# The last of 64 graphs: its transpose moved to TensorE, its steps put in a new order, its result stored by row tile

## The chip, the cores and the metric

One core of a Trainium2 chip. The metric is the device time of one execution in microseconds (us). Times below are medians of 3 to 9 executions. "Span" is the time from the first to the last instruction in the one execution that was profiled; the device time of that same execution is about 1.8 us longer.

## The reference, cut to what matters

64 graphs of 256 nodes with 512 features, f32. Two layers, each with a residual and a layer norm. In the second, a softmax over the 256 nodes of a graph scales the rows of `v`.

```python
def _L0_gnn_ref(x, adj, W):
    deg = jnp.sum(adj, axis=-1, keepdims=True)
    agg = jnp.einsum('bij,bjf->bif', adj, x) / jnp.maximum(deg, EPS)
    cat = jnp.concatenate([x, agg], axis=2)
    return jax.nn.relu(jnp.einsum('bnf,of->bno', cat, W))

def _L1_gnn_ref(X, adj, mask, Wqk, Wv):
    q, k = jnp.split(X @ Wqk, 2, axis=-1)
    v = X @ Wv
    agg = jnp.einsum('bij,bjd->bid', adj, k * mask[:, :, None])
    w = inv_scale * mask * jnp.einsum('bid,bid->bi', q, agg)
    return jax.nn.softmax(w, axis=1)[:, :, None] * v

x = _layernorm(x + _L0_gnn_ref(x, adj, L0_gnn_W), axis=-1)
x = _layernorm(x + _L1_gnn_ref(x, adj, nodemask, L1_gnn_Wqk, L1_gnn_Wv), axis=-1)
```

## The kernel before

Each product of matrices is done in Strassen's way with 7 block products (A11B11, A12B21, S1T1, S2T2, S3T3, S4B22, A22T4) in place of 8. The graphs are pipelined: in iteration i the first layer of graph i, the gather with the adjacency of graphs i and i-1, and the second layer's products of graph i-2 are woven together; graph i-4 is finished. The second layer needs the normalized rows `x1` transposed. That is done by 32x32 block transposes on VectorE and 16 small transfers that put the blocks in place:

```python
    def transpose_rows(src, dst):
        sq = pool.tile([P, P // Q, NF, NT, Q], F32, name="sq", bufs=1)
        for t in range(NT):
            nc.vector.transpose(sq[:, :, :, t, :].rearrange("p b c q -> p c b q"), src[:, t, :])
        to = dst.rearrange("f c (t a q) -> f (c t) a q", t=NT, q=Q)
        for a in range(P // Q):
            for b in range(P // Q):
                nc.sync.dma_start(to[b * Q:(b + 1) * Q, :, a, :],
                                  sq[a * Q:(a + 1) * Q, b].rearrange("p c t q -> p (c t) q"))

    def layer1_steps(g):
        # ... seven products; the first one is copied to q by ScalarE before its dot,
        #     the scores are complete only with the sixth (A22T4):
        u = bank()
        product(u, s["A11"], w["B11"])
        nc.scalar.copy(q, u)
        dot(q, 0, part)
        # ... S1T1, S2T2, A12B21, S3T3 ...
        product(u, s["A22"], w["T4"], start=False)
        dot(u, 1, sc[:, 1:2])
        product(p5, s["S4"], w["B22"], start=False)
        nc.vector.tensor_add(v[:, 0, :], p5, v[:, 0, :])

    def finish(g):
        x1, v, p = x1s.pop(g), vs.pop(g), probs.pop(g)
        o = pool.tile([P, NT, F], F32, name="o")
        for t in range(NT):
            nc.vector.scalar_tensor_tensor(o[:, t, :], v[:, t, :], p[:, t:t + 1], x1[:, t, :],
                                           op0=OP.mult, op1=OP.add)
        layer_norm(o, o)
        nc.sync.dma_start(out[g].rearrange("(t p) f -> p t f", p=P), o)

    for i in range(B + LAG - 1):
        # ...
        if i - 3 >= B - 2:            # the last two graphs: scores turned by TensorE, softmax on one row
            softmax_turned(i - 3)
            finish(i - 3)
        # ...
```

In all other iterations the 16 transfers have time: those of graph 61 are issued from 1886.82 to 1897.22 us, and its `x1T` is first read at 1909.0, without a wait. For graph 63, the last, nothing is left to do meanwhile.

Of the kernel before, what the change touches and what calls it, by code (L numbers as in the profile page):

```python
# [35 lines left out]
F32 = mybir.dt.float32  # L36
AF = mybir.ActivationFunctionType
OP = mybir.AluOpType
AX = mybir.AxisListType

P = 128
Q = 32
LAG = 4
# [5 lines left out]
def resnorm_kernel(  # L49
# [12 lines left out]
    nc = tc.nc  # L62
    B, N, F = x.shape
    A = wqk_t.shape[0] // 2
    NT, NF, NA = N // P, F // P, A // P
    H, HF = NF // 2, F // 2
# [5 lines left out]
    pool = ctx.enter_context(tc.tile_pool(name="pool", bufs=2))  # L72
    small = ctx.enter_context(tc.tile_pool(name="small", bufs=4))
# [28 lines left out]
    with setup as sp:  # L102
        wqk = sp.tile([P, 2 * NA, F], F32, name="wqk")
        for a in range(NA):
            src = wqk_t.rearrange("(h a p) f -> a p h f", p=P, h=2)[a]
# [14 lines left out]
        ident = const.tile([P, P], F32, name="ident")  # L120
        make_identity(nc, ident)
        eps = const.tile([P, 1], F32, name="eps")
# [23 lines left out]
    def row_sums(aT, eng):  # L146
# [8 lines left out]
        eng.tensor_sub(s4, a12, s2)  # L155
        return {"A11": a11, "A12": a12, "A22": a22, "S1": s1, "S2": s2, "S3": s3, "S4": s4}

    def product(ps, a, b, start=True):
        for c in range(H):
            nc.tensor.matmul(ps, a[:, c, :], b[:, c, :], start=start and c == 0, stop=(c == H - 1),  # L160
                             skip_group_check=True)

    def bank():
        return ps_mm.tile([P, F], F32, name="mm")
# [11 lines that stand above are left out]
                                  sq[a * Q:(a + 1) * Q, b].rearrange("p c t q -> p (c t) q"))  # L176

    def layer_norm(src, dst):
        mv = small.tile([P, NT, 2], F32, name="mv")
        for t in range(NT):  # L180
            st = small.tile([P, 6], F32, name="st")
            nc.vector.bn_stats(st, src[:, t, :])  # L182
            nc.vector.bn_aggr(mv[:, t, :], st)  # L183
        rstd = small.tile([P, NT], F32, name="rstd")
        nc.scalar.activation(rstd, mv[:, :, 1], AF.Ln, bias=eps)  # L185
        nc.scalar.activation(rstd, rstd, AF.Exp, scale=-0.5)
        for t in range(NT):
            nc.vector.tensor_scalar(dst[:, t, :], src[:, t, :], mv[:, t, 0:1], rstd[:, t:t + 1],  # L188
                                    op0=OP.subtract, op1=OP.mult)

# [105 lines left out]
    def norm0(g):  # L296
        x1s[g] = pool.tile([P, NT, F], F32, name="x1", bufs=LAG + 2)
        layer_norm(owns.pop(g), x1s[g])
        for t in range(NT):
            nc.scalar.activation(values(g + 1)[:, 1, t, :], x1s[g][:, t, :], AF.Copy,  # L300
                                 scale=mask_sb[:, t, g:g + 1])
        x1Ts[g] = pool.tile([P, NF, N], F32, name="x1T")
        transpose_rows(x1s[g], x1Ts[g])

    def turn(g):
        sums1[g] = row_sums(x1Ts.pop(g), nc.vector)
# [1 line left out]
    def layer1_steps(g):  # L308
        sc, part = scores[g] = (small.tile([P, NT], F32, name="scores", bufs=3),
                                small.tile([P, 1], F32, name="part", bufs=3))  # L310
        s, w, agg = sums1.pop(g), W1, aggs.pop(g + 1)[:, 1]
        v = vs[g] = late.tile([P, NT, F], F32, name="v", bufs=LAG)
        q = pool.tile([P, F], F32, name="q")

        def dot(a, t, to):
            nc.vector.scalar_tensor_tensor(q, a, 1.0, agg[:, t, :], op0=OP.mult, op1=OP.mult, accum_out=to)  # L316
# [5 lines that stand above are left out]
        yield  # L322
        p5 = bank()
        product(p5, s["S1"], w["T1"])
        yield
        product(u, s["S2"], w["T2"], start=False)
        nc.scalar.copy(v[:, 0, :], u)  # L327
        yield
        p2 = bank()
        product(p2, s["A12"], w["B21"])  # L330
        dot(p2, 0, sc[:, 0:1])
        yield
        product(u, s["S3"], w["T3"], start=False)
        nc.scalar.copy(v[:, 1, :], u)  # L334
        nc.vector.tensor_add(v[:, 1, :], p5, v[:, 1, :])
        yield
        product(u, s["A22"], w["T4"], start=False)
        dot(u, 1, sc[:, 1:2])
        yield
        product(p5, s["S4"], w["B22"], start=False)  # L340
        nc.vector.tensor_add(v[:, 0, :], p5, v[:, 0, :])  # L341
        yield

    def scale_scores(g, to):
        w, part = scores.pop(g)
        nc.vector.tensor_add(w[:, 0:1], w[:, 0:1], part)
        nc.vector.scalar_tensor_tensor(to, w, inv_scale, mask_sb[:, :, g], op0=OP.mult, op1=OP.mult)

    def write_scores(g):
# [12 lines left out]
    def softmax(g):  # L362
        w, row = columns.pop(g), rowsW.pop(g)
        top = small.tile([P, 1], F32, name="top")
        nc.vector.reduce_max(top, row, axis=AX.X, negate=True)
        total = small.tile([P, 1], F32, name="total")
        nc.scalar.activation(row, row, AF.Exp, bias=top, accum_out=total)
        p = probs[g] = small.tile([P, NT], F32, name="probs", bufs=2)
        nc.scalar.activation(p, w[:, :NT], AF.Exp, bias=top)
        nc.vector.reciprocal(total, total)  # L370
        nc.vector.tensor_scalar(p, p, total, None, op0=OP.mult)

    def softmax_turned(g):
        w = small.tile([P, NT], F32, name="w", bufs=2)
        scale_scores(g, w)
        wr = bank()[:1, :N]
        for t in range(NT):
            nc.tensor.transpose(wr[:, t * P:(t + 1) * P], w[:, t:t + 1], ident)
        top = small.tile([1, 1], F32, name="top1", bufs=2)
        nc.vector.reduce_max(top, wr, axis=AX.X, negate=True)  # L380
        e = small.tile([1, N], F32, name="e", bufs=2)
        total = small.tile([1, 1], F32, name="total1", bufs=2)
        nc.scalar.activation(e, wr, AF.Exp, bias=top, accum_out=total)
        nc.vector.reciprocal(total, total)
        nc.vector.tensor_scalar(e, e, total, None, op0=OP.mult)
        ps = bank()[:, :NT]
        for t in range(NT):
            nc.tensor.transpose(ps[:, t:t + 1], e[:, t * P:(t + 1) * P], ident[:1, :1])
        probs[g] = small.tile([P, NT], F32, name="probs", bufs=2)
        nc.vector.tensor_copy(probs[g], ps)  # L390

    def finish(g):
        x1, v, p = x1s.pop(g), vs.pop(g), probs.pop(g)
# [6 lines that stand above are left out]
# [4 lines left out]
        for _ in range(n):  # L404
            next(gen, None)

    for i in range(B + LAG - 1):
        new = i < B
        if i + 2 < B:
            with tc.issue_after(loaded.ins):  # L410
                loaded = load(i + 2)
        if i == 1:
            W1 = weight_sums(w1, "t1_")
        if 0 <= i - 3 < B - 2:
            write_scores(i - 3)
            read_scores(i - 3)
        if new:
            began, added = layer0_a(i)
        if 0 <= i - 2 < B:
            turn(i - 2)  # L420
        l1 = layer1_steps(i - 2) if 0 <= i - 2 < B else iter(())
        step(l1)
        if new:
            layer0_b(i)
        if i - 3 >= B - 2:
            softmax_turned(i - 3)
            finish(i - 3)
        if i <= B:
            z, summed = gather_a(i)
        step(l1, 2)  # L430
        step(z)
        if 0 <= i - LAG < B - 2:
            with tc.issue_after(began.ins), tc.issue_after(added.ins):
                softmax(i - LAG)
            with tc.issue_after(summed.ins):
                finish(i - LAG)
        for _ in range(4):
            step(l1)
            step(z)
        if new:  # L440
            combine0(i)
            norm0(i)
        if i + 1 < B:
            with tc.issue_after(began.ins), tc.issue_after(added.ins):
                prepare(i + 1)
# [26 lines left out]
```

## Time and profile before

| what | before |
|---|---|
| device time, median of the first 3 runs | 1988.32 us (1986.9 to 1988.72); in all later comparisons medians of 1987.68 to 1988.52 |
| span of the profiled run | 1986.5 us |
| TensorE busy | 99% |
| part of the span that the change can reach | the last 43 us |

How to read the lines in this document. A timeline line has start (us), length (us), engine, source line, operation, output<-input, shapes, count of instructions merged into it; in brackets the idle time of the engine just before it and what ended it. PE is TensorE, PEld its weight loads, DVE VectorE, ACT ScalarE, POOL GpSimd, SPq the queue that issues transfers. One f32 block product shows as two MATMUL instructions, so a Strassen product of two blocks is "x4". Numbers of source lines are those of the kernel that ran: L160 of the kernel before is L162 of the changed one.

For the end of the kernel I count from the start of the last gather's first product (`mm<-vals,adj`, at 1945.97 here), and call that "after the gather". The kernel before: last product ends at 29.6, last combination of softmax and residual starts at 32.4, end at 40.5.

### The profile page before, as it was taken

What the parts mean: (1) busy time and instruction counts of PE and PEld (TensorE: products, weight loads), DVE (VectorE), ACT (ScalarE), POOL (GpSimd) and SP (SyncE); (2) the same over time, 40 slices, a digit from 0 to 9 for tenths busy, and PEclk for the clock granted to TensorE, in tenths of its full rate; (3) what the DMA queues carried; (4) which work ended last, traced back from release to release, by engine and by line L of the source; (5) the groups of instructions that cost most, each with busy time, mean ns of one, the idle gap of its engine ahead of it and who ended that gap; (6) DMA issues with size and microseconds to landing.
All of it is one profiled execution on the core that took longest, in us unless ns stands there. A gap on an engine that the chain in (4) does not pass through costs nothing.

```text
span 1986.5 us, 19676 instructions
## 1 busy us (share of the span) xinstructions
PE 1960.3 (99%) x5416; PEld 1017.5 (51%) x5416; DVE 1566.5 (79%) x3218; ACT 650.0 (33%) x1543; POOL 419.6 (21%) x518
## 2 busy tenths in 40 slices
PE   8999999999999999999999999999999999999996
PEld 3554555555555545555555555555555555555552
DVE  5677877888788788778878887887787788878877
ACT  2323333333233333333332333333333333323332
POOL 3122221221221221222212212212222122122100
PEclk9999999999999999999999999999999999999999
DMA  6333333333333333333333333333333333333221
GB/s 223 88 83 82 98 94 85 95 91 90 96 80 100 93 83 103 93 81 95 91 90 95 83 98 94 83 102 93 81 95 92 89 96 81 101 96 80 80 45 56
DMA packets 394830, 182.62 MB, mean 92 GB/s; under 512 B 285793, under 2 KB 359393, under 8 KB 394721
## 3 DMA queue, kind: packets, MB, share of 16 engines
q1 hardware_dynamic: 394720, 181.36, 34.0%
q8 instruction: 44, 0.72, 0.2%
q14 instruction: 66, 0.53, 0.1%
HBM read 114.10 MB, written 33.62 MB: 74 GB/s over the span
## 4 chain that ended last, share of the span: by engine, by line
PE 96%; DVE 1%; SPq 1%; DMA 0%; ACT 0%; issue 0%; DVEq 0%
PE mm L160 76%; PE mm L259 19%; SPq L175 1%; PE mm L131 1%; DVE st L182 0%; DMA adj<-adj_t 0%; DMA wqk<-wqk_t 0%; DVE own L293 0%; DVE own L291 0%; DMA x1T<-sq 0%; DVE x L188 0%; DVE o L396 0%; ACT vals L300 0%; DVE v L341 0%; DVE t L141 0%
## 5 line engine op out<-in xcount | busy, mean ns | idle before, releaser
L160 PE MATMUL mm<-w,s 128*128 128x512 f32 x1024 | 481.5, 592 | 0.8 <-ACT v L327 0.8
L160 PE MATMUL mm<-t,s 128*128 128x512 f32 x1024 | 461.4, 593 | 0.2 <-ACT q L320 0.2
L160 PEld LDWEIGHTS mm<-t,s 128*128 128x128 f32 x1024 | 194.7, 190 | 243.7 <-issue 228.2
L160 PEld LDWEIGHTS mm<-w,s 128*128 128x128 f32 x1024 | 194.2, 190 | 192.8 <-issue 155.0
L160 PE MATMUL mm<-w,x1T 128*128 128x512 f32 x512 | 241.4, 594 | 3.9 <-DMA x1T<-sq 3.9
L160 PE MATMUL mm<-w,xT 128*128 128x512 f32 x512 | 240.9, 592 | 0.0
L201 POOL TENSOR_TENSOR sa<-adj 128x128 f32<-128x128 f32 x64 | 45.8, 716 | 760.2 <-PE mm L259 758.7
L152 POOL TENSOR_TENSOR s<-xT 128x256 f32<-128x256 f32 x64 | 46.8, 731 | 706.3 <-PE mm L160 687.3
L259 PE MATMUL mm<-tv,sa 128*128 128x256 f32 x768 | 187.4, 379 | 0.6 <-DVE tv L249 0.4
L259 PEld LDWEIGHTS mm<-tv,sa 128*128 128x128 f32 x768 | 145.7, 190 | 76.3 <-issue 48.2
L233 DVE TENSOR_TENSOR vals<-mm,vals 128x512 f32<-128x512 f32 x64 | 44.2, 691 | 142.9 <-PE mm L160 142.9
L185 ACT ACTIVATE rstd<-mv,eps 128x2 f32<-128x2 f32 x128 | 37.9, 296 | 341.3 <-DVE mv L183 341.3
L160 PEld LDWEIGHTS mm<-w,x1T 128*128 128x128 f32 x512 | 97.2, 190 | 98.9 <-issue 95.6
L160 PEld LDWEIGHTS mm<-w,xT 128*128 128x128 f32 x512 | 97.3, 190 | 94.7 <-issue 91.4
L327 ACT COPY v<-mm 128x512 f32<-128x512 f32 x64 | 37.5, 586 | 284.8 <-PE mm L160 284.8
L160 PE MATMUL mm<-t,xT 128*128 128x512 f32 x256 | 126.8, 617 | 2.8 <-ACT vals L222 2.8
L160 PE MATMUL mm<-t,x1T 128*128 128x512 f32 x256 | 125.4, 612 | 0.9 <-ACT v L334 0.9
L291 DVE SCALAR_TENSOR_TENSOR own<-zr,rdeg,own 128x512 f32<-128x512 f32 x128 | 107.6, 841 | 22.0 <-ACT zr L281 21.9
L259 PE MATMUL mm<-vals,adj 128*128 128x256 f32 x512 | 121.3, 379 | 1.9 <-DVE vals L233 1.9
L259 PEld LDWEIGHTS mm<-vals,adj 128*128 128x128 f32 x512 | 97.1, 190 | 43.6 <-issue 16.7
L215 ACT COPY own<-mm 128x512 f32<-128x512 f32 x64 | 37.5, 586 | 227.4 <-PE mm L160 227.4
L316 DVE SCALAR_TENSOR_TENSOR q<-mm,zr 128x512 f32<-128x512 f32 x128 | 86.1, 673 | 32.4 <-PE mm L160 32.4
(89 smaller groups left out, 2729.5 us busy)
## 6 DMA issues: line engine op xcount, KB each, us to landing
xT<-x_t SPq DMA_DIRECT2D x64, 512.0 KB
x<-x SPq DMA_DIRECT2D x64, 512.0 KB
x1T<-sq SPq DMA_DIRECT2D x1024, 32.0 KB
out<-o SPq DMA_DIRECT2D x64, 512.0 KB
adj<-adj_t SPq DMA_DIRECT2D x64, 256.0 KB
rows<-adj SPq DMA_DIRECT2D x64, 256.0 KB
row<-d SPq DMA_DIRECT2D x62, 128.0 KB
d<-turned SPq DMA_DIRECT2D x248, 0.2 KB
```

Of the source, the lines that this page charges most:

```text
L131: nc.tensor.matmul(ps[c], wqk[:, a, c * P:(c + 1) * P], wqk[:, NA + a, :], start=(a == 0), stop=(a == NA - 1))
L152: eng.tensor_add(s1, a21, a22)
L160: nc.tensor.matmul(ps, a[:, c, :], b[:, c, :], start=start and c == 0, stop=(c == H - 1), skip_group_check=True)
L175: nc.sync.dma_start(to[b * Q:(b + 1) * Q, :, a, :], sq[a * Q:(a + 1) * Q, b].rearrange("p c t q -> p (c t) q"))
L185: nc.scalar.activation(rstd, mv[:, :, 1], AF.Ln, bias=eps)
L201: nc.gpsimd.tensor_add(sa[:, 0], a21, a22)
L215: began = nc.scalar.copy(own[:, 0, :], u)
L233: nc.vector.tensor_add(y[:, 0, :], p5, y[:, 0, :])
L259: nc.tensor.matmul(ps[:, k * HF:(k + 1) * HF], sumsA[g - k][a], w[b][:, n, :], start=start and n == 0, stop=True, skip_group_check=True)
L291: nc.vector.scalar_tensor_tensor(own[:, t, :], z[:, t, :], rdeg[:, t:t + 1], own[:, t, :], op0=OP.mult, op1=OP.add)
L316: nc.vector.scalar_tensor_tensor(q, a, 1.0, agg[:, t, :], op0=OP.mult, op1=OP.mult, accum_out=to)
L327: nc.scalar.copy(v[:, 0, :], u)
```

## The change

Its intent: let TensorE transpose the last x1 so that no transfer is waited for; do the products that the scores need first (A11B11, A12B21, S2T2, A22T4, S3T3), so that the softmax runs beside the rest; normalize and store the last two row tiles one by one.

```diff
@@ norm0
         x1Ts[g] = pool.tile([P, NF, N], F32, name="x1T")
-        transpose_rows(x1s[g], x1Ts[g])
+        if g < B - 1:
+            transpose_rows(x1s[g], x1Ts[g])
+
+    def turn_last(g):
+        for t in range(NT):
+            ps = bank()
+            for c in range(NF):
+                nc.tensor.transpose(ps[:, c * P:(c + 1) * P], x1s[g][:, t, c * P:(c + 1) * P], ident)
+            copy = nc.scalar.copy if t else nc.vector.tensor_copy
+            copy(x1Ts[g][:, :, t * P:(t + 1) * P], ps.rearrange("p (c n) -> p c n", c=NF))
@@ new
+    def layer1_last(g):
+        # ... set-up, dot() cut
+        u, p2, p3, p4, p5 = (bank() for _ in range(5))
+        product(u, s["A11"], w["B11"])
+        dot(u, 0, part[:, 0:1])
+        with tc.issue_after(queued[0]):
+            e = softmax_rows(g - 1)
+        product(p2, s["A12"], w["B21"])
+        dot(p2, 0, sc[:, 0:1])
+        with tc.issue_after(queued[0]):
+            probs[g - 1] = softmax_cols(e)
+        finish(g - 1)
+        product(u, s["S2"], w["T2"], start=False)
+        nc.scalar.copy(v[:, 0, :], u)
+        product(p4, s["A22"], w["T4"])
+        dot(p4, 1, part[:, 1:2])
+        product(u, s["S3"], w["T3"], start=False)
+        dot(u, 1, sc[:, 1:2])
+        nc.scalar.copy(v[:, 1, :], u)
+        product(p3, s["S4"], w["B22"])
+        with tc.issue_after(queued[0]):
+            e = softmax_rows(g)
+        nc.vector.tensor_add(v[:, 0, :], p3, v[:, 0, :])
+        product(p5, s["S1"], w["T1"])
+        for t in range(NT):
+            nc.vector.tensor_add(v[:, t, :], p5, v[:, t, :])
+        with tc.issue_after(queued[0]):
+            p = softmax_cols(e)
+        for t in range(NT):
+            ot = o[:, t:t + 1, :]
+            nc.vector.scalar_tensor_tensor(ot[:, 0], v[:, t, :], p[:, t:t + 1], x1[:, t, :],
+                                           op0=OP.mult, op1=OP.add)
+            layer_norm(ot, ot)
+            nc.sync.dma_start(out[g, t * P:(t + 1) * P, :], ot[:, 0])
@@ main loop (cut): one iteration fewer; turn_last(B - 1) in iteration B, layer1_last(B - 1) in iteration B + 1
```

In the build that ran, the scheduler put S3T3 ahead of A22T4. Not shown: `product` remembers its last instruction in `queued`, `layer_norm` takes one tile or two, `softmax_turned` is cut into `softmax_rows` and `softmax_cols`.

More of the change, by code (lines that the diff above doesn't have):

```diff
@@ L156, in row_sums @@
         return {"A11": a11, "A12": a12, "A22": a22, "S1": s1, "S2": s2, "S3": s3, "S4": s4}
+    queued = [None]
     def product(ps, a, b, start=True):
         for c in range(H):
-            nc.tensor.matmul(ps, a[:, c, :], b[:, c, :], start=start and c == 0, stop=(c == H - 1),
-                             skip_group_check=True)
+            queued[0] = nc.tensor.matmul(ps, a[:, c, :], b[:, c, :], start=start and c == 0,
+                                         stop=(c == H - 1), skip_group_check=True).ins
     def bank():
@@ L178, in layer_norm @@
     def layer_norm(src, dst):
+        n = src.shape[1]
         mv = small.tile([P, NT, 2], F32, name="mv")
-        for t in range(NT):
+        for t in range(n):
             st = small.tile([P, 6], F32, name="st")
@@ L184, in layer_norm @@
         rstd = small.tile([P, NT], F32, name="rstd")
-        nc.scalar.activation(rstd, mv[:, :, 1], AF.Ln, bias=eps)
-        nc.scalar.activation(rstd, rstd, AF.Exp, scale=-0.5)
-        for t in range(NT):
+        nc.scalar.activation(rstd[:, :n], mv[:, :n, 1], AF.Ln, bias=eps)
+        nc.scalar.activation(rstd[:, :n], rstd[:, :n], AF.Exp, scale=-0.5)
+        for t in range(n):
             nc.vector.tensor_scalar(dst[:, t, :], src[:, t, :], mv[:, t, 0:1], rstd[:, t:t + 1],
@@ L342, in layer1_steps, with dot @@
         yield
+    def layer1_last(g):
+        sc, part = scores[g] = (small.tile([P, NT], F32, name="scores", bufs=3),
+                                small.tile([P, NT], F32, name="parts", bufs=1))
+        s, w, agg, x1 = sums1.pop(g), W1, aggs.pop(g + 1)[:, 1], x1s.pop(g)
+        v = late.tile([P, NT, F], F32, name="v", bufs=LAG)
+        o = pool.tile([P, NT, F], F32, name="o")
+        q = pool.tile([P, F], F32, name="q")
+        def dot(a, t, to):
+            nc.vector.scalar_tensor_tensor(q, a, 1.0, agg[:, t, :], op0=OP.mult, op1=OP.mult, accum_out=to)
+        u, p2, p3, p4, p5 = (bank() for _ in range(5))
[30 more added lines that the diff above has]
+            nc.sync.dma_start(out[g, t * P:(t + 1) * P, :], ot[:, 0])
     def scale_scores(g, to):
         w, part = scores.pop(g)
-        nc.vector.tensor_add(w[:, 0:1], w[:, 0:1], part)
+        n = part.shape[1]
+        nc.vector.tensor_add(w[:, :n], w[:, :n], part)
         nc.vector.scalar_tensor_tensor(to, w, inv_scale, mask_sb[:, :, g], op0=OP.mult, op1=OP.mult)
@@ L371, in softmax, with softmax_rows @@
         nc.vector.tensor_scalar(p, p, total, None, op0=OP.mult)
-    def softmax_turned(g):
+    def softmax_rows(g):
         w = small.tile([P, NT], F32, name="w", bufs=2)
@@ L385, in softmax_turned, with softmax_cols @@
         nc.vector.tensor_scalar(e, e, total, None, op0=OP.mult)
+        return e
+    def softmax_cols(e):
         ps = bank()[:, :NT]
@@ L388, in softmax_turned @@
             nc.tensor.transpose(ps[:, t:t + 1], e[:, t * P:(t + 1) * P], ident[:1, :1])
-        probs[g] = small.tile([P, NT], F32, name="probs", bufs=2)
-        nc.vector.tensor_copy(probs[g], ps)
+        p = small.tile([P, NT], F32, name="probs", bufs=2)
+        nc.vector.tensor_copy(p, ps)
+        return p
     def finish(g):
@@ L405, in step @@
             next(gen, None)
-    for i in range(B + LAG - 1):
+    for i in range(B + LAG - 2):
         new = i < B
@@ L420, in resnorm_kernel @@
             turn(i - 2)
-        l1 = layer1_steps(i - 2) if 0 <= i - 2 < B else iter(())
+        l1 = layer1_steps(i - 2) if 0 <= i - 2 < B - 1 else iter(())
         step(l1)
@@ L424, in resnorm_kernel @@
             layer0_b(i)
-        if i - 3 >= B - 2:
-            softmax_turned(i - 3)
-            finish(i - 3)
+        if i - 3 == B - 2:
+            with tc.issue_after(summed.ins):
+                softmax(i - LAG)
+                finish(i - LAG)
+            layer1_last(B - 1)
         if i <= B:
@@ L431, in resnorm_kernel @@
         step(z)
-        if 0 <= i - LAG < B - 2:
+        if 0 <= i - LAG < B - 3:
             with tc.issue_after(began.ins), tc.issue_after(added.ins):
@@ L436, in resnorm_kernel @@
                 finish(i - LAG)
+        if i == B:
+            with tc.issue_after(queued[0]):
+                turn_last(B - 1)
         for _ in range(4):
```

## The prediction

The sum stands as it was forecast: 4.1 us, 4.0 after the price of the transposes, so 1984.3, and 1984.5 with 0.2 net for rival (a). Cut are (a)'s comparison of its wait with an idle time that no run had shown, and the terms of rival (b); the 1.6 us upward in the range is (a)'s 0.9 with the cut term of (b). That 0.9 and its chance of a third are estimates: the slow products of the trace are 0.77 and 0.59 us longer than warm ones. So is the 0.22 us for a transpose, from the measured pace of 0.215 us.

> **What bounds the kernel now.** I read the page first, then the chain that ended last, then the last 40 us in order of time.
>
> ```profile
> PE 1960.3 (99%) x5416; PEld 1017.5 (51%) x5416; DVE 1566.5 (79%) x3218; ACT 650.0 (33%) x1543; POOL 419.6 (21%) x518
> PE 96%; DVE 1%; SPq 1%; DMA 0%; ACT 0%; issue 0%; DVEq 0%
> ```
>
> TensorE is busy for 99% of the span and carries 96% of the chain. The change does not touch its 64 graphs of matmuls: the order of instructions of the changed build is the same on all engines until graph 63, the last, has been normalized by its first layer, about 1943.4 us into a span of 1986.5. So at most the last 43 us, 2.2% of the span, can move, and most of that is work that stays. The stretches there (busy time of each engine, count, clock, DMA share, GB/s):
>
> ```profile
> core 0: us, PE busy (x) PEld busy (x) DVE busy (x) ACT busy (x) POOL busy (x), PEclk, DMA share, GB/s
> 1945.00:1959.50 14.50, 10.42 (x30) 5.50 (x30) 10.11 (x27) 3.57 (x9) 0.00 (x0) 1.00 0.27 50
> 1959.50:1975.90 16.40, 15.43 (x34) 5.75 (x34) 12.98 (x35) 3.51 (x10) 0.00 (x0) 0.90 0.17 62
> 1975.90:1986.50 10.60, 0.29 (x3) 0.20 (x2) 5.24 (x13) 1.06 (x4) 0.00 (x0) 0.75 0.23 86
> ```
>
> Three losses: TensorE idle for 4 of the first 14.5 us; a clock of 0.90 in the second stretch; no matmul at all in the last 10.6 us. The timeline names them:
>
> ```profile
> 1944.95 1.29 DVE L171 STREAM_TRANSPOSE sq<-x 128x512 f32<-128x512 f32 x2
> 1946.31 11.59 SPq L175 DMA_DIRECT2D x1T<-sq  x16
> 1955.08 0.59 PE L259 MATMUL mm<-vals,sa 128*128 128x256 f32 x2
> 1959.55 2.65 PE L160 MATMUL mm<-w,x1T 128*128 128x512 f32 x4 [3.87 <-DMA x1T<-sq]
> 1962.87 2.57 PE L160 MATMUL mm<-t,s 128*128 128x512 f32 x4 [0.25 <-ACT q L320]
> 1967.40 1.88 PE L160 MATMUL mm<-w,x1T 128*128 128x512 f32 x4
> 1971.67 1.98 PE L160 MATMUL mm<-t,x1T 128*128 128x512 f32 x4 [0.68 <-ACT v L334]
> 1973.63 1.98 PE L160 MATMUL mm<-w,s 128*128 128x512 f32 x4
> 1975.65 0.69 DVE L341 TENSOR_TENSOR v<-mm,v 128x512 f32<-128x512 f32 x1 [0.17 <-PE mm L160]
> 1978.38 1.41 DVE L396 SCALAR_TENSOR_TENSOR o<-v,probs,x 128x512 f32<-128x512 f32 x2
> 1981.81 1.00 DVE L188 TENSOR_SCALAR o<-o,mv,rstd 128x512 f32<-128x512 f32 x2 [0.60 <-ACT rstd L186]
> ```
>
> The transpose of x1 goes through VectorE and 16 small transfers, issued in 11.59 us; TensorE runs out of other work at 1955.67 and waits 3.87 us. Then eight matmul instructions take 2.65 and 2.57 us where the same form takes 1.88 warm: (2.65-1.88)+(2.57-1.98) = 1.4 us, and the two small transposes among them 0.64 against 0.38, so some 1.6 us of slow clock. At the end VectorE and ScalarE work alone: from the last matmul's end at 1975.61, softmax, normalization and store take 10.9 us.
>
> [...]3.87 us of idle, then slow matmuls. [...]No full f32 block is transposed here before; the nearest row is a 128x128 weight load, 190 ns, at a pace of 0.215 us where 256-column matmuls follow it. [...]The chain shows 1.95 us from the last x1T issue to its landing, and 3.69 us from the last normalization's end (1982.81) to the end of the span, of which about 1.4 move the 512 KB.
>
> **The change part by part.** I took the new order of each engine and its waits and added durations from the trace, from 1944.24 (TensorE has its last product before the part that differs). The same addition of the old order lands within 0.1 us of the trace at 1955.7, and again from the end of the slow clock to the last normalization, so the method is good to about that.
>
> 1. Removed: the two VectorE transposes (1.29 us), the 16 issues, the 3.87 us wait, the 1.6 us of slow clock, and one ScalarE copy (0.59).
> 2. Added on TensorE: 8 transposes. With 0.22 us each[...], 1.8 us at 1946.7, behind the two gather products (1945.85 to 1946.7), fully on TensorE's path. The copies out, one on VectorE (taken as the 0.69 of an addition from PSUM) and one on ScalarE (0.59), lie beside the next product and gathers: VectorE's ends at 1950.7, and the first product of the last graph wants it at 1952.3.
> 3. The products now follow without a gap. From 1948.4: graph 62's product (2 x 0.86), gathers and remaining products of 62 with half a product of 63 to 1957.4 (small waits for ScalarE's copies, 0.1 to 0.3), rest of that product, scores of 62 turned at 1958.3, then A12B21 and S2T2 to 1961.95.
> 4. New waits on TensorE. The product S3T3 adds into the bank that ScalarE copies first: copy at 1962.1, start at 1962.75, 0.8 us lost. Then it waits for the scaled exponentials of 62 (0.3, at 1964.9). Then S4B22 is streamed by 1968.55, and the next instruction in its order, the turn of 63's scores, waits for VectorE. VectorE still has graph 62 to finish: probabilities at 1965.4, two combinations (0.66 each to the next), statistics (0.60 each), a dot (0.60), the v addition, two normalizations (0.45 each), the second dot (0.67), two small ones; scores at 1971.3. TensorE stands 2.8 us.
> 5. The last product S1T1 then runs 1971.6 to 1973.45 beside the maximum, exponential and scaling of 63's scores (done 1973.3). Before, its counterpart ended at 1975.61: 2.2 us earlier.
> 6. From the last product: two additions of 0.61 and a copy to 1974.9 (the small transposes of e are ready before), two combinations to 1976.3, statistics to 1977.5, aggregates to 1977.7, ScalarE twice two small ones (one more pair than before, half overlapped) to 1978.35, normalizations ending 1978.9 and 1979.4. That is 5.9 us where the old chain took 7.2 (1975.61 to 1982.81): the first combination starts 1.4 us after the last product in place of 2.8, and from there on the two are equal.
> 7. Stores by row tile: the first 256 KB leave 0.45 us before the second, and the last transfer carries half: of the 3.69 us tail I take off 0.6 (an estimate: half of the 1.4 us of moving).
>
> Sum: 2.2 + 1.3 + 0.6 = 4.1 us. The transposes at 0.22 rather than the 0.21 that I added with cost 0.1. The span was 1986.5 where the median is 1988.32, so 1.8 us lie outside it, taken as unchanged: 1988.3 - 4.0 = 1984.3.
>
> **The rivals.** (a) Slow clock at the new wait. [...]If the clock falls, the last product takes up to 0.9 us longer and its end is on the path: about 1985.1. I weigh this with a third, +0.3 us. The old trace speaks for a drop only after 3.87 us, and against one after the 0.68 at 1971.67. (b) The transposes cost more than a weight load each[...] (c) VectorE takes the place of the DMA as the bound: already in step 4, as 12 us of nearly unbroken VectorE from 1958.5 to 1971.3; any VectorE row 10% longer adds up to 1 us. (d) Nothing is gained, because the 3.87 us wait just moves behind graph 62's finish: 1988. Against it: the addition has 63's products start 7 us earlier, at 1952.3 against 1959.55, and the wait left is 2.8. (e) More is gained, if VectorE's queue of graph 62 waits less than I think: the floor is TensorE's work without waits, about 3.5 us less: 1981.
>
> **Range and chances.** From (a) I add 0.2 net: predicted 1984.5. Runs before spread over 1.8 us; (a) and (b) together could put it 1.6 up, (e) some 2 down. 1982.3 to 1986.7 should hold it 8 times in 10. Two per cent is 40 us, about all that is not shared work, so within 2%: 0.985; faster 0.01, slower 0.005.
>
> **What would show each step.** Transposes at 0.22 us in a row at about 1946.7 and no x1T transfer in the last 40 us (1, 2); no TensorE wait over 1 us between 1948 and 1962, clock 1.00 there (3); a wait of 2 to 3.5 us before the turn of the last scores, released by VectorE, and the shorter one for ScalarE's v copy (4); about 6 us from the last product to the last normalization (6); about 3.1 from there to the end (7). Wrong would be: slow matmuls after the transposes[...], or a store tail that stays at 3.7.

## The result, and the profile after

The change took 1983.99 us (median of 6 runs, 1983.78 to 1984.69) where the kernel before took 1988.52 (6 runs, 1986.9 to 1990.27). The ratio is 0.9978 (95% interval 0.9965 to 0.999). Ratios here are the mean time of one kernel's runs over that of the other's of the same rounds, so not quite the ratio of these medians. That is 4.5 us, 0.2%: "the same" by a threshold of 2%, but clear of noise.

The page of the changed kernel, busy time and chain:

```profile
PE 1959.8 (99%) x5424; PEld 1018.5 (51%) x5424; DVE 1566.7 (79%) x3220; ACT 650.0 (33%) x1545; POOL 419.4 (21%) x518
PE 98%; DVE 1%; DMA 0%; ACT 0%; issue 0%; DVEq 0%
```

The transfer queue (SPq) has left the chain. The same stretches as in the prediction (the last one ends with the span):

```profile
1945.00:1959.50 14.50, 14.50 (x49) 8.11 (x48) 13.48 (x36) 4.47 (x13) 0.00 (x0) 1.00 0.10 38
1959.50:1975.90 16.40, 11.23 (x26) 4.03 (x24) 12.45 (x34) 2.96 (x10) 0.00 (x0) 0.90 0.17 64
1975.90:1982.80 6.90, 0.00 (x0) 0.00 (x0) 3.20 (x8) 0.71 (x4) 0.00 (x0) 0.62 0.20 76
```

TensorE (first pair of numbers) now fills the first stretch and has gaps in the second, whose clock is 0.90 again. The last stretch, without products, went from 10.6 to 6.9 us. The timeline, in the same places as before:

```profile
1946.38 1.04 PE L313 MATMUL mm<-ident,x 128*128 128x128 f32 x8
1951.13 1.02 PE L162 MATMUL mm<-w,x1T 128*128 128x512 f32 x2
1961.63 1.98 PE L162 MATMUL mm<-w,s 128*128 128x512 f32 x4 [0.68 <-ACT v L379]
1970.25 0.38 PE L436 MATMUL mm<-ident,w 128*1 128x128 f32 x2 [2.69 <-DVE w L405]
1970.47 3.37 PE L162 MATMUL mm<-t,s 128*128 128x512 f32 x4
1973.88 1.29 DVE L391 TENSOR_TENSOR v<-mm,v 128x512 f32<-128x512 f32 x2 [1.64 <-PE mm L162]
1975.27 1.42 DVE L396 SCALAR_TENSOR_TENSOR o<-v,probs,x 128x512 f32<-128x512 f32 x2
1978.60 1.00 DVE L191 TENSOR_SCALAR o<-o,mv,rstd 128x512 f32<-128x512 f32 x2 [0.51 <-ACT rstd L189]
```

All 8 transposes take 1.04 us. The wait for transfers is gone. A wait of 2.69 us for the last scores has come, and the product behind it takes 3.37 us instead of 1.88: the clock fell here too (0.50 granted from 1970.71 to 1974.13 us). The end comes 37.3 us after the gather, not 40.5.

### The profile page after: what moved, and what is told of

Same layout as the page of the kernel before. It is cut to its first block, busy times and chain, and to the rows that moved or that the text cites. A ratio compares the mean times of both kernels' runs of the same rounds, so it can differ in the third digit from the quotient of the medians.

```text
span 1982.8 us, 19678 instructions
## 1 busy us (share of the span) xinstructions
PE 1959.8 (99%) x5424; PEld 1018.5 (51%) x5424; DVE 1566.7 (79%) x3220; ACT 650.0 (33%) x1545; POOL 419.4 (21%) x518
## 4 chain that ended last, share of the span: by engine, by line
PE 98%; DVE 1%; DMA 0%; ACT 0%; issue 0%; DVEq 0%
PE mm L162 77%; PE mm L262 19%; PE mm L131 1%; DMA wqk<-wqk_t 0%; DMA adj<-adj_t 0%; DVE st L185 0%; ACT vals L303 0%; DVE own L296 0%; ACT vals L225 0%; DVE o L396 0%; DVE vals L236 0%; DVE own L223 0%; DVE t L141 0%; DVE t L140 0%; DVE w L142 0%
## 5 line engine op out<-in xcount | busy, mean ns | idle before, releaser
L262 PEld LDWEIGHTS mm<-vals,adj 128*128 128x128 f32 x512 | 97.1, 190 | 43.6 <-issue 16.9
L328 DVE SCALAR_TENSOR_TENSOR q<-mm,zr 128x512 f32<-128x512 f32 x126 | 84.7, 672 | 32.4 <-PE mm L162 32.4
```

The costliest lines, as they stand in the source:

```text
L262: nc.tensor.matmul(ps[:, k * HF:(k + 1) * HF], sumsA[g - k][a], w[b][:, n, :], start=start and n == 0, stop=True, skip_group_check=True)
L328: nc.vector.scalar_tensor_tensor(q, a, 1.0, agg[:, t, :], op0=OP.mult, op1=OP.mult, accum_out=to)
```

## The experiments

Twelve runs, each with 5 timed runs, in three groups that share 9 runs of the kernel before: medians 1987.68 (first four), 1987.82 (next four), 1988.12 (last four). All gave correct results. Two theories were there first. A: the gain is the transfer wait and its slow clock, and the new order brings nothing. B: both parts gain, as the prediction adds them up. Theories C (an idle wait lets the clock fall, which costs what follows) and D (VectorE sets the time of the last scores) came from the profile after.

The table gives what the profiles show, in us after the gather: the start of the instruction that scales the last scores, the end of the last Strassen product, the start of the last combination, the end. Each number is a difference of two starts or ends in the timelines.

| kernel | scores | last product ends | combination | end | median time | ratio |
|---|---|---|---|---|---|---|
| before | 29.4 | 29.6 | 32.4 | 40.5 | 1987.7 to 1988.5 | |
| the change (first run, clock fell) | 24.5 | 28.3 | 29.8 | 37.3 | 1983.99 | 0.9978 |
| the change again (clock stayed) | 24.5 | 26.8 | 28.3 | 35.8 | 1984.34 | 0.9982 |
| transposes alone | 24.3 | 24.6 | 27.4 | 35.4 | 1982.86 | 0.9976 |
| order and stores alone | 24.7 | 27.1 | 28.5 | 36.0 | 1984.64 | 0.9983 |
| change, one store | 24.5 | 27.5 | 28.9 | 37.0 | 1984.46 | 0.9984 |
| change, transposes x4 | 24.3 | 26.6 | 28.0 | 35.6 | 1983.66 | 0.9979 |
| change, kept warm | 24.5 | 26.9 | 28.4 | 35.9 | 1983.51 | 0.9979 |
| change, VectorE relieved | 23.5 | 25.8 | 27.3 | 34.9 | 1982.76 | 0.9975 |
| relieved, S1T1 early | 23.5 | 23.7 | 26.5 | 34.1 | 1982.57 | 0.9971 |
| before, kept warm | 28.3 | 28.6 | 31.4 | 39.4 | 1986.40 | 0.9992 |
| transposes and stores | 24.3 | 24.6 | 27.4 | 34.9 | 1982.41 | 0.9973 |
| the same, relieved | 23.4 | 24.4 | 27.2 | 34.8 | 1982.64 | 0.9973 |
| change, S1T1 early | 25.6 | 23.8 | 28.4 | 35.9 | 1983.56 | 0.9979 |

The intervals of the ratios are about 0.0013 to each side, mostly from the spread of the kernel before (1985.6 to 1990.3), so neighbouring ratios are not told apart by them; the profiles and the ranges of the kernels' own runs are what tells.

### turn_only: the transposes alone

```diff
 # the kernel before
-        transpose_rows(x1s[g], x1Ts[g])
+        if g < B - 1:
+            transpose_rows(x1s[g], x1Ts[g])
 ...
+        if i == B:
+            with tc.issue_after(queued[0]):
+                turn_last(B - 1)
```

> The kernel before with one part of the change: x1 of the last graph transposed by TensorE and copied out by VectorE and ScalarE, the last graph's steps and store as before. Theory A (the wait for the transfers and the slow clock after it are the whole gain; the new order of the last graph brings nothing of its own): the 3.87 us wait and the slow matmuls go, no TensorE wait of over 1 us comes before the last scores, the last normalization ends some 5 us earlier than 1982.8, span 1981 to 1982, at least as fast as the whole change (1982.8). Theory B (both parts gain, as the prediction has it): the gain is 2 to 3 us, span near 1984, behind the whole change.

Measured: 1982.86 us (1982.41 to 1983.7), span 1980.8. That is Theory A's number (its span was to be 1981 to 1982), and faster than the change, whose 11 runs in other rounds lie between 1983.72 and 1984.69. The ratios of the two (0.9976, and 0.9978 and 0.9982) are not told apart; by the profiles it ends 0.4 us before the change with its clock up (35.4 and 35.8 after the gather). The timeline, TensorE and VectorE of the last part:

```profile
1968.02 1.98 PE L162 MATMUL mm<-w,s 128*128 128x512 f32 x4
1969.92 0.38 PE L389 MATMUL mm<-ident,w 128*1 128x128 f32 x2
1972.77 1.41 DVE L407 SCALAR_TENSOR_TENSOR o<-v,probs,x 128x512 f32<-128x512 f32 x2
```

In the old order TensorE reaches the turn of the last scores with no wait that the trace lists, and no product comes behind it.

### order_only: the new order and the stores, without the transposes

```diff
 # the change
-        if g < B - 1:
-            transpose_rows(x1s[g], x1Ts[g])
+        transpose_rows(x1s[g], x1Ts[g])
 ...
-        if i == B:
-            with tc.issue_after(queued[0]):
-                turn_last(B - 1)
```

> The whole change except that x1 of the last graph still goes through VectorE and the 16 transfers. Theory A: the wait of nearly 4 us and the slow clock stay; products that start after 1959 leave no room; the span is within 1 us of 1986.5, the last stores by tile being worth about half a us. Theory B: half of the gain is here, span 1984 to 1985, because the softmax lies beside the rest. In both the wait before the last scores shrinks from 2.7 to under 1 us, since TensorE comes later.

Measured: 1984.64 us, but from 1983.01 to 1986.17, a spread of 3.2 us where most kernels here spread by 1 to 2. The span of that median run is 1982.9 us, less than either theory expected (A within 1 us of 1986.5, B 1984 to 1985). So A is wrong in its second half: the order does bring something, where the transfers stay. The profiled run was one of the fast ones, with a span of 1981.2:

```profile
1958.67 1.95 PE L162 MATMUL mm<-w,x1T 128*128 128x512 f32 x4 [3.81 <-DMA x1T<-sq]
1960.68 1.88 PE L162 MATMUL mm<-w,x1T 128*128 128x512 f32 x4
1970.11 0.38 PE L435 MATMUL mm<-ident,w 128*1 128x128 f32 x2 [0.20 <-DVE w L404]
```

After a wait of 3.81 us the products ran at full pace here (1.95 and 1.88 us, granted clock 1.00 from 1958 to 1970), though the same wait of 3.87 us was followed by slow ones in the kernel before (2.65 and 2.57 us, clock 0.76 from 1959 to 1966). TensorE started late, then had no wait over 0.2 us, and reached the scores at 24.7 us after the gather: only 0.2 later than the change, although the products began 8 us later than in it (13.5 against 5.6). The two parts of the change buy the same time. Each alone brings the last scores from 29.4 to 24.3 or 24.7; together to 24.5. About 1.1 of these 5 us is the clock, which stayed up here: the kernel before has them at 28.3 where it is kept warm (before_warm, below).

### one_store: the last graph stored in one piece

```diff
 # the change
-        for t in range(NT):
-            ot = o[:, t:t + 1, :]
-            ...combination of tile t...
-            layer_norm(ot, ot)
-            nc.sync.dma_start(out[g, t * P:(t + 1) * P, :], ot[:, 0])
+        for t in range(NT):
+            ...combination of tile t...
+        layer_norm(o, o)
+        nc.sync.dma_start(out[g].rearrange("(t p) f -> p t f", p=P), o)
```

> The change with its last graph normalized and stored in one piece. If the stores by tile are worth what the prediction said (half of the moving of 512 KB, 0.6 us, less the extra small ScalarE instructions of about 0.15): the time from the last normalization to the end goes from 3.2 to 3.7 us and the span is 0.3 to 0.5 us longer. Rival[...]: 3.2 us stay, and the span is 0.1 to 0.2 us shorter.

Measured: from the last normalization to the end 3.62 us, against 3.20 and 3.18 in the two profiles of the change. The time was 1984.46, and that is 0.1 to 0.5 over the change in other rounds, too little to call. The stores by tile are worth 0.4 us by the trace, and turn_only and turn_tile below, which differ only in this, end 0.5 us apart (35.4 and 34.9). Its last product, with the same code as the change up to there, took 2.57 us.

### turn_x4: each transpose done four times

```diff
-            for c in range(NF):
+            for c in range(4 * NF):
+                c = c % NF
```

> The change with each of the 8 transposes done four times into the same place (the scheduler also puts the product A22T4 before S3T3). If the transposes are on the path that sets the end, as the prediction has it, 24 more at 0.11 us make the span 2.6 us longer, 1985.4. Rival (TensorE has slack from the 2.7 us wait for the last scores and VectorE is the bound): the wait shrinks from 2.7 to about 1 us, the clock does not fall, and the span is within 0.8 us of 1982.8 or even shorter.

Measured: 1983.66 us, not longer than the change. The timeline:

```profile
1947.19 3.66 PE L314 MATMUL mm<-ident,x 128*128 128x128 f32 x32
1970.80 0.38 PE L437 MATMUL mm<-ident,w 128*1 128x128 f32 x2 [0.85 <-DVE w L406]
```

24 more transposes cost 2.62 us of TensorE (3.66 less 1.04), and the wait for the last scores shrank from 2.69 to 0.85 us. It looks as if this work was not on the path that sets the end, but the chains that ended last, of the change and of this run, say otherwise. The transposes lie on both:

```profile
1946.55 0.87 PE mm L313 x8
1947.35 3.49 PE mm L314 x32
```

What hid the 2.62 us is the scheduler, which moved A22T4 ahead of S3T3. The wait of 0.68 us for ScalarE's copy and the 1.98 us of S3T3 then no longer stand before the turn of graph 62's exponentials, which starts 18.0 us after the gather, as in the change (18.1). So the run does not say what 24 transposes cost in the unchanged order.

### after_again: the change unedited

> The change itself, unedited, beside the next three: 1983.8 to 1984.7 as in its first runs, about 0.998 of before. Its profile again has a wait of 2.7 us before the last scores are turned; whether the last product then takes 1.9 us (warm) or 2.5 to 3.4 (cold) may differ from run to run.

Measured: 1984.34 us (1983.72 to 1984.46). The profiled run had the same wait as the first, and a warm last product:

```profile
1970.86 0.38 PE L436 MATMUL mm<-ident,w 128*1 128x128 f32 x2 [2.70 <-DVE w L405]
1971.07 1.88 PE L162 MATMUL mm<-t,s 128*128 128x512 f32 x4
1974.38 1.42 DVE L396 SCALAR_TENSOR_TENSOR o<-v,probs,x 128x512 f32<-128x512 f32 x2
```

The clock granted between 1970 and 1975 us was 0.66 in the first profile and 1.00 in this one. With the product 1.49 us shorter (3.37 less 1.88), the last combination came 1.49 us earlier after the gather (29.75 less 28.26). One kernel, two endings: up to the start of the last product the two timelines agree to 0.01 us after the gather, and from there nothing differs but the clock. The timed runs, which have no trace, don't say which of them paid it.

The clock of the two endings, two stretches of the first profile of the change and one of this profile (the first number after the comma is TensorE's busy time, the third from the end the clock):

```profile
1970.00:1975.00 5.00, 3.89 (x8) 1.34 (x8) 2.19 (x7) 0.99 (x3) 0.00 (x0) 0.66 0.28 105
1970.71:1974.13 3.42, 3.42 (x6) 0.96 (x4) 1.11 (x4) 0.56 (x2) 0.00 (x0) 0.50 0.23 88
1970.00:1975.00 5.00, 2.32 (x8) 0.96 (x8) 3.61 (x11) 1.14 (x3) 0.00 (x0) 1.00 0.28 105
```

In the first profile the clock fell 0.46 us after the end of the wait (1967.56 to 1970.25), with the last product under way. Here it did not fall after a wait of the same length (1968.16 to 1970.86). So the length of a wait alone does not part the cases: after 2.69, 2.69 and 2.70 us the product took 3.37, 2.57 (one_store) and 1.88 us, and the 3.81 us of order_only were followed by warm products, the 3.87 us of the kernel before by slow ones. What does part them is not shown.

### warm: TensorE kept busy in its wait

```diff
         product(p3, s["S4"], w["B22"])
+        spare = bank()
+        for n in range(3):
+            with tc.issue_after(queued[0]):
+                queued[0] = nc.tensor.matmul(spare, w["B11"][:, 0, :P], w["B11"][:, 1, :], ...).ins
         with tc.issue_after(queued[0]):
             e = softmax_rows(g)
```

> The change with three extra matmuls (results unused) between the product S4B22 and the turn of the last scores, to keep TensorE busy in its 2.7 us wait. Theory C (the idle wait lets the clock fall, and the last product, 3.37 us in place of 1.9, then sets the end): the last product takes 1.9 to 2.0 us, the last normalization ends at once 1 to 1.4 us earlier, median about 1982.8. Rival (the last product is slow for another reason, or its length is hidden behind the softmax on VectorE): the extra matmuls change nothing, within 0.3 us of the change.

Measured: 1983.51 us (1982.89 to 1984.66), 0.8 under the change in the same rounds, where about 1982.8 was expected, 1.5 under it. The last product:

```profile
1967.04 2.74 PE L389 MATMUL mm<-w 128*128 128x512 f32 x6
1970.21 1.88 PE L162 MATMUL mm<-t,s 128*128 128x512 f32 x4
```

It is warm (1.88 us), as in the second profile of the change, and the end after the gather is the same (35.9 and 35.8). The medians are in line with a cost of the clock in some runs of the change, not in all; with ranges that overlap, this run alone does not prove it.

### relief: part of VectorE's work for graphs 61 and 62 on GpSimd

```diff
-    def layer_norm(src, dst):
+    def layer_norm(src, dst, eng=nc.vector):
 ...
-            nc.vector.tensor_scalar(dst[:, t, :], src[:, t, :], ...)
+            eng.tensor_scalar(dst[:, t, :], src[:, t, :], ...)
 ...  # in finish(g)
-        layer_norm(o, o)
+        layer_norm(o, o, nc.gpsimd if g >= B - 3 else nc.vector)
```

> The change with the last step of normalization (subtract and multiply, two tiles) of graphs 61 and 62 moved from VectorE to GpSimd. Theory D (VectorE's work for graph 62 is what TensorE waits for, 2.7 us): the wait shrinks by the 0.9 us taken off, to about 1.8, the clock stays up more often, and the median falls by 1.2 (still cold) to 2.5 us, to 1981.5 to 1982.8. Rival (the wait is set by TensorE's or ScalarE's results that VectorE waits for): the wait stays at 2.5 us or more and the time within 0.3 us of the change.

Measured: 1982.76 us (1982.47 to 1983.81), 1.6 under the change. The wait and the moved work:

```profile
1969.18 4.13 POOL L191 TENSOR_SCALAR o<-o,mv,rstd 128x512 f32<-128x512 f32 x2 [0.83 <-ACT rstd L189]
1970.32 0.38 PE L436 MATMUL mm<-ident,w 128*1 128x128 f32 x2 [1.78 <-DVE w L405]
```

The wait fell from 2.70 to 1.78 us, by the 0.9 that VectorE was relieved of, though GpSimd needs 4.13 us (a span that is rough in the profile) for what VectorE did in 1.00. Theory D holds: VectorE's work for graph 62 is what TensorE waits for. The product after the wait was warm (1.88) in this profile; whether it is in every execution is not shown.

### early and early_relief: no product behind the scores

```diff
         product(p3, s["S4"], w["B22"])
+        product(p5, s["S1"], w["T1"])
         with tc.issue_after(queued[0]):
             e = softmax_rows(g)
         nc.vector.tensor_add(v[:, 0, :], p3, v[:, 0, :])
-        product(p5, s["S1"], w["T1"])
```

> The change with the product S1T1 before the turn of the last scores, nothing moved to GpSimd. TensorE then has no product after its wait, so a fallen clock costs nothing, but VectorE's two additions of that product come before the scores and delay them by up to 1.1 us. Expected: the last combination starts 28.3 us after the last gather's first product, the same as the change when its clock does not fall (28.26), 1.5 us under the change when it does (29.75); median 0 to 0.8 us under the change. If VectorE had slack there, 27.2.

> The one before, and the last product S1T1 put before the turn of the last scores, so that no product follows the wait. Theories C and D together: no product is left to run cold, VectorE's additions of it lie in the waits for the exponential, wait of TensorE below 0.5 us; last normalization some 3 us earlier than in the change, median 1980.5 to 1981.5. If C and D are wrong: within 0.5 us of the change. This is also the candidate for a version that beats both kernels.

("The one before" in the second text is relief.) Measured for the first: 1983.56 us (1982.85 to 1984.69), combination at 28.4 after the gather, as expected to 0.1: the scores came 1.0 later (25.6), because VectorE did the two additions of S1T1 ahead of them. Moving TensorE's work does not help while VectorE is the bound. With VectorE relieved as well (early_relief): 1982.57 us (1981.52 to 1982.76), ratio 0.9971, combination at 26.5, end at 34.1. The median is 1.1 us above the upper end of what I expected (1980.5 to 1981.5), though the end after the gather is 3.2 us earlier than in the first profile of the change, as expected; this profiled run reached the gather late (1946.80).

### before_warm: TensorE kept busy in the transfer wait of the kernel before

```diff
 # the kernel before, start of layer1_steps for the last graph
+        if g == B - 1:
+            spare = bank()
+            for n in range(4):
+                with tc.issue_after(queued[0]):
+                    queued[0] = nc.tensor.matmul(spare, w["B11"][:, 0, :P], w["B11"][:, 1, :], ...).ins
```

> The kernel before with four extra matmuls (eight instructions, 3.4 us, results unused) that TensorE runs while it waits for the 16 transfers. Theory C (the idle wait lets the clock fall): no slow matmuls follow, the end comes up to 1.6 us earlier relative to the last gather (38.9 to 39.3 us after its first product in place of 40.5), and the runs spread less; median 1.0 to 1.6 us under before. The transfer wait itself stays. Rival (the slow matmuls come from the transfers or the loads, not from idleness): they stay, and the median is that of before.

Measured: 1986.40 us (1985.58 to 1986.69), 1.7 under the kernel before in the same rounds, which spread from 1985.59 to 1990.27. The profile:

```profile
1954.71 3.60 PE L324 MATMUL mm<-w 128*128 128x512 f32 x8
1958.92 1.95 PE L162 MATMUL mm<-w,x1T 128*128 128x512 f32 x4 [0.62 <-issue]
1961.55 1.98 PE L162 MATMUL mm<-t,s 128*128 128x512 f32 x4 [0.46 <-ACT q L328]
```

The first products of the last graph start as late as before (13.8 us after the gather, 13.6 in the kernel before), but take 1.95 and 1.98 us and not 2.65 and 2.57. Theory C agrees with that for the kernel before: with useless work in the wait the granted clock was 1.00 from 1959 to 1966, where it was 0.76, and that is worth 1.1 us in the profile (end at 39.4, 0.1 later than expected). The 1.7 us of the medians are no proof of it: the interval of the ratio, 0.9978 to 1.0006, includes no gain. It may also be why the kernel before and order_only, which both wait nearly 4 us, spread more than the others; the timed runs have no trace, so that is not shown.

### turn_tile and turn_tile_relief: the change less its new order

```diff
 # turn_only, in finish(g)
+        if g == B - 1:
+            for t in range(NT):
+                ...combination of tile t...
+                layer_norm(ot, ot)
+                nc.sync.dma_start(out[g, t * P:(t + 1) * P, :], ot[:, 0])
+            return
```

> The kernel before with TensorE's transposes and the stores by row tile, the order of the last graph as before: the change less its new order. If the new order is worth nothing once the transfers are gone (Theory A): the end 35.0 to 35.3 us after the last gather's first product, 0.3 us under the run with the transposes alone, and median 1982.4 to 1983.0, at least 0.8 under the change. If the order helps (Theory B): slower than the change.

> The one before, with the last step of normalization of graphs 61 and 62 on GpSimd. In the old order TensorE reaches the last product only just before VectorE reaches the scores, so VectorE's relief (0.9 us) is worth 0.3 us at most: end 34.8 to 35.0 us after the last gather's first product. If VectorE alone were the bound in this order too, 34.2.

Measured: 1982.41 us (1981.61 to 1983.37) and 1982.64 (1981.87 to 1983.0). The profile of the first ends 34.9 us after the gather, 0.1 below what was expected, and 0.8 us before the change with its clock up:

```profile
1968.70 1.98 PE L162 MATMUL mm<-w,s 128*128 128x512 f32 x4
1970.60 0.38 PE L390 MATMUL mm<-ident,w 128*1 128x128 f32 x2
```

So, by the profiles, the new order is worth less than nothing once TensorE transposes; the medians (1982.41, and 1983.99 and 1984.34 in other rounds) point the same way. In the old order the last product is over at 24.6 and VectorE needs one addition after it. In the new order it starts only after the scores are turned, ends at 26.8 at best, and VectorE adds twice: the combination then starts 3.7 us after the scaling of the scores, not 3.1. Relieving VectorE brings the scores 0.9 earlier in the old order too (23.4), but only 0.2 of that reaches the combination, since there the last product (24.4) is the later one.

Two kernels are the fastest by their medians: turn_tile, 1982.41 us (ratio 0.9973), which is the change without its largest part, and early_relief, 1982.57 (0.9971). By their times they are not told apart; by the profile early_relief ends 0.8 us earlier after the gather (34.1 and 34.9).

## Why the prediction was right or wrong

The predicted time, 1984.5 us, is 0.5 us from the measured one. From the gather to the end of the span its times give 36.6 us, and the two profiles of the change 37.3 and 35.8: it lies between two endings of the same kernel, and that the median lies so near is in part luck. The prediction's own times, put on the same scale (it had the gather at 1945.85), against the two profiles of the change:

| step | predicted, after the gather | measured |
|---|---|---|
| transposes end, next product starts (2) | 2.55 | 1.74 |
| first product of the last graph (3) | 6.4 | 5.6 |
| S3T3 starts after waiting for ScalarE (4) | 16.9, waited 0.8 | 16.1, waited 0.68 |
| turn of the last scores (4) | waited 2.8 | waited 2.69 and 2.70 |
| last product (5) | 25.7 to 27.6 | 25.0 to 28.3 and 25.0 to 26.8 |
| last combination (6) | 29.0 | 29.8 and 28.3 |
| last normalization ends (6) | 33.5 | 34.1 and 32.6 |
| from there to the end (7) | 3.1 | 3.20 and 3.18 |

- Step 1 was right in its mechanism and nearly in size: the transfer wait and the slow clock are gone, and the profile of before_warm gives 1.1 us for the slow clock, where 1.6 was worked out. What the prediction did not see is that such a wait need not cost the clock: the one of 3.81 us in order_only was followed by products of 1.95 and 1.88 us at a granted clock of 1.00.
- Step 2 had the path right and the price wrong. "With 0.22 us each" was twice too much: the 8 took 1.04 us in all, 0.11 to 0.13 each. The row that the estimate came from, 190 ns for a weight load, is that of an f32 product; the weight loads of the transposes took 142 ns on average. What sets the pace of 0.11 us no run shows. "Fully on TensorE's path" agrees with the chain of the changed kernel, which holds all 8 transposes for 0.87 us; turn_x4 can't test it, since its order changed too.
- Step 3, no gap between 1948 and 1961: right, all of the first stretch is busy.
- Step 4, the two waits that replace the old one: right to 0.1 us each, in size and in what releases them; relief shows the cause. The third wait, 0.3 for the exponentials of 62, did not come: TensorE had just got there (the turn of e started at 1963.65, 0.06 after they were scaled).
- Steps 5 and 6: the length of the last product is the term that went wrong. It was taken as warm, with a third of a chance of 0.9 us more. It took 1.9, 2.6 and 3.4 us in three profiles of the same code up to there. A miss of up to 1.5 us, in the direction of rival (a), and the 0.8 us by which the overpriced transposes put everything late (2.55 against 1.74) cancels about half of it. The total was closer than its terms. What the prediction held against rival (a), that the old trace shows a drop only after 3.87 us, was the wrong test: waits of 2.69 us were enough in two profiles.
- Step 7: right, and a little oversized. One store in place of two costs 0.4 us; the prediction took 0.6.
- What the prediction never asked is what each part brings alone; its sum is one for the whole change. By the medians of the same rounds the transposes alone give 4.8 us (1987.68 less 1982.86), the order and stores alone 3.0, and both together 4.5 and 3.5 in their two sets of rounds, not 7.8. The parts don't add up. Rival (c) names the reason in the new order, VectorE becoming the bound, and the prediction did not ask what then is left of the order's worth.

The range held, and the chances too: with 98% of the span untouched, there was little doubt about "within 2%".

What stays open: what parts the waits after which the clock falls from the others; how often it falls in the timed runs, which have no trace; and what more transposes cost in the unchanged order. Not tried: VectorE's own order. S3T3, which the last dot needs, ends 18.1 us after the gather, and VectorE starts that dot at 23.6, behind graph 62's normalization.

## What to carry to other kernels

When a change has two parts that buy the same time, try each alone: after the first one another engine may be the bound (here VectorE, in the new order), and the second may cost. At the end of a kernel, don't leave a product behind a wait: if the clock falls after the wait, the product pays for it (here 3.37 us in place of 1.88), and one profile may show it and the next not. When a run is meant to test whether work lies on the path, look for that work on the chain too: a scheduler may have moved other work to make room. A row of a profile gives the cost of an operation only for the same kind of use; a weight load for an f32 product and one for a transpose took 190 and 142 ns.
